# Placing the expert choices of layer 1's second sequence behind the multiplication of its cosines

## The chip, the core and the metric

The kernel runs on one core of one Trainium2 chip. The metric is the device time of that core in microseconds (us). All data are float32. The core has TensorE (PE in the profile, with PEld for its weight loads), VectorE (DVE), ScalarE (ACT), GpSimd (POOL) and SyncE (SP); each works through a stream of instructions in order, and waits at an instruction until the data and the buffers that it needs are there. SP issues loads and stores, POOL the gathers and scatters.

## The reference, cut to what matters

The input x is 4 sequences of 1024 tokens of width 256. Two layers follow one another, each of the same outer form:

```python
xn = layernorm(x)
s = attn(xn)                    # layer 0: a gated recurrence; layer 1: the attention below
x = x + s * silu(ffn(xn))
```

Layer 1's attention and its feed-forward part are

```python
proj = cos(theta) * cos(xn)                       # theta: one angle per column
attn = softmax(proj @ proj.T / 4)                 # per sequence
s = (attn @ proj) @ W_c.T + b_c

shared = (silu(xn @ sg.T) * (xn @ su.T)) @ sd.T   # 512 hidden columns
scores = sigmoid(xn @ router.T)                   # 16 experts in 4 groups
# two best groups by the sum of their two best scores, four best experts within
idx, w = topk(scores masked to those groups, 4);  w = w / sum(w)
routed = sum over the four: (w * silu(xn @ gate_e) * (xn @ up_e)) @ down_e   # 64 hidden columns
ffn = shared + routed
```

Layer 0's feed-forward part has 16 routed experts of 128 hidden columns, four per token, and no shared expert.

## The kernel before, in words

**Tiles.** A sequence is 8 tiles of 128 tokens, or two halves (q = 0, 1) of 512. Buffers come from pools of fixed size: "x" has 8 (gathered rows r, weighted sums y, layer 1's val, the dispatch's t_half), "t" has 1, "act" and "sg" 4, "o" 3; PSUM has four rings of two banks, "mm", "gu", "tp" and "acc". An instruction that takes a buffer waits for the last reader of what lay in it.

**Routed experts.** Tokens are scattered by POOL into rows sorted by expert (rows_in), the experts run over fixed blocks of these rows, and their results are gathered back. Layer 0's experts run over all sequences, in two groups of halves: (0,0), (0,1), (1,0) and (1,1), (2,0), (2,1), (3,0), (3,1), written (sequence, half). After them comes the combine (gated0, L773): per tile, a "piece": POOL gathers four rows per token (L730), DVE adds them weighted (one L795 of 0.25 to 0.35 us and three L797), and after four pieces ACT and DVE apply silu (L473, L474), DVE multiplies by the recurrence's output (L804) and adds to x (L806), and SP stores the half. So 12 pieces belong to the first group and 20 to the second.

**Layer 1 per sequence b.**
- route1(b) (L913), for each half that the combine has finished: layernorm statistics on DVE (L197, L198), the reciprocal root by Newton steps (L206 to L214), the scaling on ACT (L231), eight transposes on PE (L240), their copies into xnT (L242 on DVE, L244 on ACT), and a store of the normalized half to normed (SP). For b = 2 and 3 also a store of the transposed sequence to normedT. Then the router's products (L301), sigmoid (L317 on ACT), and about 40 small DVE instructions that choose the experts (L318 to L351, the choices), copies of the choices (em, L933) and of the normalized weights (L358 to L361, L934).
- places1(h) (L364 and what follows) for a pair of sequences: two PE products over the choices (L375, L377) and DVE instructions L381 to L448, which give each token its rows. There are two pairs, (0,1) and (2,3).
- dispatch1(h) (L943): POOL loads the normalized halves (L958), copies their places beside them (L959, L960) and scatters them (64 L587 for each pair).
- prep1(b) (L974): in four blocks of 512 columns, five DVE instructions each reduce the angles (L175 to L184, the cosine blocks); ACT takes the sine (L1002); DVE multiplies by cos(theta) (L1005, twice), which makes projT; PE multiplies by W_c into val (L1013, 16 products in PSUM "gu"), which ACT copies out (L1020). For b below 2 it uses the transposed tile that route1 left in `turned[b]`; for b = 2 and 3 it waits until route1(b) is emitted (`routed_done`) and loads normedT.
- attend(b) (L1025): scores L1066 in "mm", transposes L1074 where a block mirrors one already taken, ACT exponentials (L1078, L1082), products with val (L1098 in "acc"), then eviction of each half (sv, L1123 on DVE and a copy on ACT) and scaling (L1040, L1041, L1045).
- share(b) (L1134): products g in "mm" and u in "gu" (L1145), ACT and DVE (L473, L474, L1155), down products (L1161), eviction and store.
- experts1: the routed experts over both pairs, evictions L690, results stored by POOL (L1212); after them the rest of the layer.

**Order.** All these are generators. The main line (L1396 on) emits attend(0), share(0), attend(1), share(1), attend(2), share(2), then the routed experts. `run` (L892) advances a modelled clock after each of their steps, and lets the generators beside it (`Beside`, L872) emit what is due by then; a `yield` gives the modelled time until the next step (PIECE is 1, SETTLED 3). `combined` goes through the combine, `preparing` through prep1(b+1) beside attend(b) and share(b), and is finished before attend(b+1). `routing` goes in one line through route1(0), route1(1), places1(0), route1(2), route1(3), places1(1), dispatch1(0), dispatch1(1). Tile's scheduler fixes from this, before the run, the order of each engine's stream and the buffers.

The profile's line numbers are those of this kernel:

Of the kernel before, what the change touches and what calls it, by code (L numbers as in the profile page):

```python
# [52 lines left out]
PIECE = 1.0  # L53
# [10 lines left out]
def two_layer_kernel(  # L64
# [28 lines left out]
    def bank(tag, bufs):  # L93
        tag = side[0] if tag == "side" else tag
        return psum.tile([P, 512], F32, tag=tag, name=tag, bufs=bufs)


    def block(dram, b, q):


        if len(dram.shape) == 4:
            return dram[b, q].rearrange("p (c d) -> p c d", c=NS)
        return dram[b].rearrange("(c p) d -> p c d", p=P)[:, q * NS : (q + 1) * NS, :]
# [143 lines left out]
    def transposed_tile():  # L247
        return work.tile([P, KC, S], F32, tag="xnT", name="xnT", bufs=3)
# [28 lines left out]
    def two_of_four(v, tag):  # L277

        m = v.shape[1] // 4
        tt = nc.vector.tensor_tensor  # L280
        pair = v.rearrange("p (n two) -> p n two", two=2)
        hi = small.tile([P, 2 * m], F32, tag=f"hi{tag}", name=f"hi{tag}", bufs=1)
        lo = small.tile([P, 2 * m], F32, tag=f"lo{tag}", name=f"lo{tag}", bufs=1)
        tt(hi, pair[:, :, 0], pair[:, :, 1], ALU.max)
        tt(lo, pair[:, :, 0], pair[:, :, 1], ALU.min)
        hi2 = hi.rearrange("p (n two) -> p n two", two=2)
        lo2 = lo.rearrange("p (n two) -> p n two", two=2)
        first = small.tile([P, m], F32, tag=f"first{tag}", name=f"first{tag}", bufs=1)
        second = small.tile([P, m], F32, tag=f"second{tag}", name=f"second{tag}", bufs=1)
        rest = small.tile([P, m], F32, tag=f"rest{tag}", name=f"rest{tag}", bufs=1)  # L290
        tt(first, hi2[:, :, 0], hi2[:, :, 1], ALU.max)
        tt(second, hi2[:, :, 0], hi2[:, :, 1], ALU.min)
        tt(rest, lo2[:, :, 0], lo2[:, :, 1], ALU.max)
        tt(second, second, rest, ALU.max)
        return first, second

    def logits(lg, at, xnT, rw, tiles=range(NT)):

        for at, c in zip(range(at, 512, E), tiles):
            for kc in range(KC):  # L300
                nc.tensor.matmul(  # L301
                    lg[:, at : at + E],
                    lhsT=xnT[:, kc, c * P : (c + 1) * P],
                    rhs=rw[:, kc, :],
                    start=(kc == 0),
                    stop=(kc == KC - 1),
                )
        spent(len(tiles) * 0.44)

    def route(lg, nt, rb, masked_low):  # L310


        shape = [P, nt, E]
        flat = "p t e -> p (t e)"
        sc = small.tile(shape, F32, tag="sc", name="sc", bufs=1)

        nc.scalar.activation(sc.rearrange(flat), lg[:, 0 : nt * E], AF.Tanh, scale=0.5)  # L317
        nc.vector.tensor_scalar(sc, sc, 0.5, 0.5, ALU.mult, ALU.add)  # L318
        sb = small.tile(shape, F32, tag="sb", name="sb", bufs=1)
        nc.vector.tensor_tensor(sb, sc, rb.unsqueeze(1).to_broadcast(shape), ALU.add)  # L320
        yield PIECE
        first, second = two_of_four(sb.rearrange(flat), "e")
        yield PIECE
        gs = small.tile([P, nt, G], F32, tag="gs", name="gs", bufs=1)
        gflat = "p t g -> p (t g)"
        nc.vector.tensor_tensor(gs.rearrange(gflat), first, second, ALU.add)
        _, least = two_of_four(gs.rearrange(gflat), "g")
        yield PIECE
        gm = yield from chosen(gs, least.unsqueeze(2), 2, G)
        yield PIECE  # L330

        yield PIECE
        four = [P, nt, G, E // G]
        grouped = "p t (g k) -> p t g k"
        nc.vector.tensor_tensor(
            sb.rearrange(grouped, g=G), sb.rearrange(grouped, g=G), gm.unsqueeze(3).to_broadcast(four), ALU.mult
        )
        if masked_low:
            pen = small.tile([P, nt, G], F32, tag="pen", name="pen", bufs=1)
            nc.vector.tensor_scalar(pen, gm, BIG, -BIG, ALU.mult, ALU.add)  # L340
            nc.vector.tensor_tensor(
                sb.rearrange(grouped, g=G), sb.rearrange(grouped, g=G), pen.unsqueeze(3).to_broadcast(four), ALU.add
            )
        yield PIECE
        top = small.tile([P, nt, 8], F32, tag="top", name="top", bufs=1)
        for c in range(nt):
            nc.vector.max(top[:, c, :], sb[:, c, :])
        yield PIECE
        em = yield from chosen(sb, top[:, :, 3:4], 4, E)
        yield PIECE  # L350
        nc.vector.tensor_tensor(sc, sc, em, ALU.mult)  # L351
        return em, sc
# [220 lines left out]
    def spent(us):  # L573

        clock[0] += us
# [332 lines left out]
    em1 = small.tile([P, B * NT, E], F32, tag="em1", name="em1", bufs=1)  # L908
    comb1 = small.tile([P, B * NT, E], F32, tag="comb1", name="comb1", bufs=1)

    x1_halves = {b: [] for b in range(B)}

    def route1(b, tag):  # L913

        xnT = transposed_tile()
        for q in range(NQ):
            while len(x1_halves[b]) <= q:
                yield PIECE
            src, dst = x1_halves[b][q]
            part = [(xnT, q, src, dst)]  # L920
            scales = yield from norm_scales(part)
            yield from norm_applied(part, scales, tag)
            nc.sync.dma_start(out=block(normed, b, q), in_=dst)
        if b >= 2:
            nc.sync.dma_start(out=normedT[b], in_=xnT.rearrange("p k s -> p (k s)"))
        lg = bank(tag, 2)
        logits(lg, 0, xnT, r1w_sb)
        yield SETTLED
        if b < 2:
            turned[b] = xnT  # L930
        em, comb = yield from route(lg, NT, r1b_sb, True)
        ts = slice(b * NT, (b + 1) * NT)
        nc.vector.tensor_copy(em1[:, ts, :], em)  # L933
        nc.vector.tensor_copy(comb1[:, ts, :], normalized(comb))  # L934
# [39 lines left out]
    def prep1(b, tag):  # L974

        if b < 2:
            while b not in turned:
                yield PIECE
            xnT = turned[b]
        else:  # L980
            while b not in routed_done:
                yield PIECE
            xnT = transposed_tile()
            nc.sync.dma_start(out=xnT.rearrange("p k s -> p (k s)"), in_=normedT[b])
            there = clock[0] + LANDING
            while clock[0] < there:
                yield PIECE
        if b == 1:

            projT = [work.tile([P, QUAD, D + INFO], F32, tag="q", name="projT", bufs=QB) for _ in range(KC)]  # L990
            projT = [t.rearrange("p i d -> p (i d)")[:, 0:S] for t in projT]
        else:
            projT = work.tile([P, KC, S], F32, tag="big_a", name="projT", bufs=1)
            projT = [projT[:, kc, :] for kc in range(KC)]
        for kc in range(KC):
            for cols in (slice(0, TB), slice(TB, S)):
                k = work.tile([P, TB], F32, tag="t", name="k", bufs=1)
                for _ in cos_reduced(projT[kc][:, cols], xnT[:, kc, cols], k, TWO_PI_NORMED):
                    pass
                yield 2 * PIECE  # L1000
        for kc in range(KC):
            nc.scalar.activation(projT[kc], projT[kc], AF.Sin, bias=half_pi, scale=-1.0)  # L1002
        yield PIECE
        for kc in range(KC):
            nc.vector.tensor_scalar(projT[kc], projT[kc], cth[:, kc : kc + 1], None, ALU.mult)  # L1005
        yield 3 * SETTLED

        val = [xpool.tile([P, NS, D + INFO], F32, tag="x", name="val", bufs=XB)[:, :, 0:D] for _ in range(NQ)]
        for c in range(0, NT, 2):
            ps = bank(tag, 2)  # L1010
            for i in range(2):
                for kc in range(KC):
                    nc.tensor.matmul(  # L1013
                        ps[:, i * D : (i + 1) * D],
                        lhsT=projT[kc][:, (c + i) * P : (c + i + 1) * P],
                        rhs=wc_sb[:, kc, :],
                        start=(kc == 0),
                        stop=(kc == KC - 1),
                    )
            nc.scalar.copy(val[c // NS][:, c % NS : c % NS + 2, :], ps.rearrange("p (c d) -> p c d", d=D))  # L1020
            spent(1.7)
            yield PIECE
        ready[b] = xnT, projT, val
# [454 lines left out]
```

## Time and profile before

| | us |
|---|---|
| median of 9 runs | 1130.91 |
| lowest, highest | 1127.82, 1137.66 |
| profiled execution | 1132.52 |
| its span | 1130.8 |
| PE busy in it | 1028.2 |
| DVE busy | 650.2 |
| POOL busy | 568.0 |
| ACT busy | 463.9 |

The mean clock granted to TensorE in the profiled execution was 0.957 of full speed. The times of the trace count from the start of its span. In it, the choices of the second sequence stand around 514 to 541 on DVE, the multiplication L1005 of its cosines at 553.31, the first pair's places until 561; attend(2) starts at 702.72 on PE, and the routed experts of layer 1 at 790.2. POOL scatters layer 1's tokens from 628.69, and stores the first result (L1212) at 800.69.

A row of a timeline has start, length, engine, line, operation, output <- inputs, shapes and count, and, where the engine was idle before it, how long and what released it. Instructions of DVE overlap by some 0.1 us, so the distance of two starts is often a little less than the length that is shown. A product of float32 matrices is two MATMUL records; a product with 512 columns takes 0.86 us and one with 256 columns 0.43 us where PE is at full clock.

### The profile page before, as it was taken

To read this page: it belongs to the slowest core of one execution; us is meant where nothing else is said; L and a number is where in the kernel's file an instruction comes from. 1 tells how busy PE (TensorE), PEld (TensorE's weight loads), DVE (VectorE), ACT (ScalarE), POOL (GpSimd) and SP (SyncE) were. 2 spreads that over 40 slices of the span, in tenths; PEclk is the share of its full clock that TensorE was granted. 3 is DMA by queue.
4 is the path that set the end of the run, shared out by engine and by line. 5 is a ranking of instruction groups with operands and counts; after the bars stand their busy time and mean duration, and the time that the engine had idled before them with its cause. 6 is when DMAs were issued, how large, how long until landed. Compare 5 with 4: busy or idle time off the path is not lost.

```text
span 1130.8 us, 16114 instructions
## 1 busy us (share of the span) xinstructions
PE 1028.2 (91%) x4928; PEld 765.7 (68%) x4928; DVE 650.2 (57%) x1928; ACT 463.9 (41%) x1028; POOL 568.0 (50%) x589
## 2 busy tenths in 40 slices
PE   5679699999898899978599999999899999999997
PEld 4255368888677688665367765776677777776675
DVE  4867953333787733158876883034723437776666
ACT  3354364444455444321332611221745555553132
POOL 1277577721770000477253677777656666765000
PEclk9868799999999999989798989999999999999999
DMA  8997679999998587987246543564556579994871
GB/s 339 401 408 260 210 204 317 335 262 276 286 344 250 159 202 185 347 256 178 76 143 208 194 165 141 199 215 143 170 171 189 184 232 358 346 314 145 274 241 38
DMA packets 118994, 264.81 MB, mean 234 GB/s; under 512 B 14208, under 2 KB 71680, under 8 KB 117632
## 3 DMA queue, kind: packets, MB, share of 16 engines
q1 hardware_dynamic: 78256, 138.79, 39.3%
q0 software_dynamic: 27264, 75.86, 20.1%
q10 hardware_dynamic: 13392, 49.14, 12.5%
q8 instruction: 43, 0.70, 0.3%
q14 instruction: 39, 0.32, 0.1%
HBM read 119.34 MB, written 144.39 MB: 233 GB/s over the span
## 4 chain that ended last, share of the span: by engine, by line
PE 67%; DVE 19%; DMA 6%; issue 3%; POOL 2%; ACT 2%; DVEq 0%; POOLq 0%; ACTq 0%
PE gu L647 15%; PE acc L672 11%; PE acc L1098 7%; PE tp L635 6%; PE gu L1145 4%; PE mm L1066 4%; DMA r<-rows_out,row 4%; PE acc L1161 3%; PE mm L1145 3%; PE tp L664 3%; PE gu L1013 2%; DVE x_half L1250 2%; PE acc L301 2%; POOL r L730 2%; PE mm L519 1%
## 5 line engine op out<-in xcount | busy, mean ns | idle before, releaser
L730 POOL DMA_INDIRECT r<-rows_out,row x128 | 133.4, 1042 | 236.8 <-issue 154.9
L647 PE MATMUL gu<-w_sb,xT 128*128 x1280 | 239.6, 330 | 1.8 <-ACT xT L639 0.9
L647 PEld LDWEIGHTS gu<-w_sb,xT 128*128 128x128 f32 x1280 | 195.0, 193 | 16.6 <-issue 2.8
L1212 POOL DMA_INDIRECT results<-o,dest x160 | 159.5, 997 | 82.3 <-issue 28.5
L672 PE MATMUL acc<-w_sb,hT 128*128 (+1 forms) x640 | 180.2, 397 | 4.0 <-ACT hT L666 4.0
L587 POOL DMA_INDIRECT rows_in<-x_half,row x128 | 136.6, 1067 | 92.7 <-DVE stats L197 44.9
L474 DVE SCALAR_TENSOR_TENSOR h<-sg,gu 128x256 f32<-128x256 f32 (+1 forms) x160 | 56.0, 351 | 161.1 <-ACT sg L473 160.2
L587 POOL DMA_INDIRECT rows_in<-t_half,row x128 | 125.8, 983 | 40.6 <-issue 38.6
L672 PEld LDWEIGHTS acc<-w_sb,hT 128*128 128x128 f32 (+1 forms) x640 | 107.4, 189 | 32.0 <-issue 15.9
L1098 PE MATMUL acc<-val,es 128*128 128x256 f32 x512 | 125.9, 388 | 0.8 <-ACT es L1078 0.8
L639 ACT COPY xT<-tp 128x512 f32<-128x512 f32 x160 | 93.6, 586 | 74.7 <-PE tp L635 72.4
L1098 PEld LDWEIGHTS acc<-val,es 128*128 128x128 f32 x512 | 95.9, 195 | 23.8 <-issue 10.1
L635 PE MATMUL tp<-ident,xs 128*128 128x128 f32 x640 | 101.0, 281 | 0.0
L473 ACT ACTIVATE sg<-gu 128x256 f32<-128x256 f32 (+1 forms) x160 | 52.9, 331 | 115.0 <-PE gu L647 108.8
L635 PEld LDWEIGHTS tp<-ident,xs 128*128 128x128 f32 x640 | 74.4, 142 | 32.5 <-issue 18.5
L690 DVE COPY o<-acc 128x512 f32<-128x512 f32 x80 | 55.0, 688 | 63.2 <-PE acc L672 62.5
L664 PE MATMUL tp<-ident,h 128*128 128x128 f32 (+1 forms) x320 | 62.4, 277 | 9.2 <-DVE h L658 6.9
L1066 PE MATMUL mm<-projT 128*128 128x512 f32 (+3 forms) x192 | 70.6, 491 | 0.0
L666 ACT COPY hT<-tp 128x256 f32<-128x256 f32 (+1 forms) x160 | 58.5, 366 | 25.3 <-PE tp L664 23.7
L1145 PE MATMUL gu<-xnT,w_sb 128*128 128x512 f32 x128 | 61.9, 606 | 5.6 <-ACT val L1020 4.3
L1145 PE MATMUL mm<-xnT,w_sb 128*128 128x512 f32 x128 | 61.0, 601 | 1.0 <-DVE act L474 1.0
L1161 PE MATMUL acc<-w_sb,act 128*128 128x256 f32 x256 | 60.0, 381 | 0.7 <-DVE act L1155 0.7
(225 smaller groups left out, 1442.8 us busy)
## 6 DMA issues: line engine op xcount, KB each, us to landing
rows_in<-zeros SPq DMA_DIRECT2D x20, 1044.0 KB, 14.1
xs<-rows_in SPq DMA_DIRECT2D x40, 512.0 KB, 7.2
rows_out<-o ACTq DMA_DIRECT2D x40, 512.0 KB, 7.0
xs<-rows_in ACTq DMA_DIRECT2D x37, 522.0 KB, 4.7
r<-results SPq DMA_DIRECT2D x32, 512.0 KB, 6.7
rows_in<-zeros SPq DMA_DIRECT2D x1, 12288.0 KB
rows_in<-zeros SPq DMA_DIRECT2D x1, 8192.0 KB, 24.1
w_sb<-in_w_dram SPq DMA_DIRECT2D x4, 1536.0 KB, 16.2
```

What stands on the lines that cost most here:

```text
L587: nc.gpsimd.indirect_dma_start(out=view, out_offset=bass.IndirectOffsetOnAxis(ap=row[:, c0 + s, k : k + 1], axis=0), in_=tokens[:, s, :], ...
L635: nc.tensor.transpose(tp[:, at : at + P], xs[:, j % per * 2 + i, kc * P : (kc + 1) * P], ident)
L639: nc.scalar.copy(xT.rearrange("p i k t -> p (i k t)"), tp)
L647: nc.tensor.matmul(ps[:, i * 2 * hid : (i + 1) * 2 * hid], lhsT=xT[:, i, kc, :], rhs=w_sb[:, bass.ds(off + kc * 2 * hid, 2 * hid)], start= ...
L664: nc.tensor.transpose(tp[0:hid, i * P : (i + 1) * P], h[:, i, :], ident)
L672: nc.tensor.matmul(ps[:, i * D : (i + 1) * D], lhsT=hT[0:hid, i * P : (i + 1) * P], rhs=w_sb[0:hid, bass.ds(expert(2 * j + i) + 4 * hid, D ...
L730: nc.gpsimd.indirect_dma_start(out=r[:, k, :], out_offset=None, in_=rows_out[g], in_offset=bass.IndirectOffsetOnAxis(ap=row[:, c, k : k + ...
L1066: nc.tensor.matmul(ps[:, at:TB], lhsT=projT[kc][:, t * P : (t + 1) * P], rhs=projT[kc][:, q * TB + at : (q + 1) * TB], start=(kc == 0), st ...
L1098: nc.tensor.matmul(av[s // 2][:, (s % 2) * D : (s % 2 + 1) * D], lhsT=es[:, s * P : (s + 1) * P], rhs=val[t // NS][:, t % NS, :], start=(t ...
L1145: nc.tensor.matmul(ps, lhsT=w[:, kc, j * P : (j + 1) * P], rhs=xr[:, kc, :], start=(kc == 0), stop=(kc == KC - 1),)
L1161: nc.tensor.matmul(ys[s // 2][:, (s % 2) * D : (s % 2 + 1) * D], lhsT=h[:, s * P : (s + 1) * P], rhs=ds1_sb[:, j, :], start=(j == 0 and s ...
L1212: nc.gpsimd.indirect_dma_start(out=views[g - G1][QUAD * q + i], out_offset=bass.IndirectOffsetOnAxis(ap=dest[:, i : i + 1], axis=0), in_=o ...
```

## The change

A set of sequences is kept whose cosines have been multiplied. route1 for the second sequence (b = 1) now stops, after its router's products, until prep1(1) has emitted its multiplication; prep1 enters b in the set there. While it stops, it yields PIECE each time it is asked. No instruction is added or removed.

```diff
+    cosines = set()
     x1_halves = {b: [] for b in range(B)}
...
         yield SETTLED
         if b < 2:
             turned[b] = xnT
+
+        while b == 1 and b not in cosines:
+            yield PIECE
         em, comb = yield from route(lg, NT, r1b_sb, True)
...
         for kc in range(KC):
             nc.vector.tensor_scalar(projT[kc], projT[kc], cth[:, kc : kc + 1], None, ALU.mult)
+        cosines.add(b)
         yield 3 * SETTLED
```

Since `routing` is one line of generators, what follows route1(1) in it also follows the multiplication: the first pair's places, route1(2) and route1(3), the second pair's places, and the dispatch; and prep1(2), which waits for route1(2). The combine is a generator of its own and does not wait. The changed kernel's line numbers are larger by 1 from L911, by 4 from L932 and by 5 from L1006; the text gives those of before.

## Prediction

> **What bounds the kernel now.** I read first the page's busy shares and the 40 slices (28.3 us each), then the table of windows over the stretch in which layer 1's second sequence is prepared, then the timelines of PE and DVE there, and last the order in which both programs' instructions stand on each engine, which the scheduler fixes before the run.
>
> ```profile
> PE 1028.2 (91%) x4928; PEld 765.7 (68%) x4928; DVE 650.2 (57%) x1928; ACT 463.9 (41%) x1028; POOL 568.0 (50%) x589
> PE   5679699999898899978599999999899999999997
> ```
> ```profile
> 520.00:540.00 20.00, 13.78 (x44) 8.62 (x43) 20.00 (x71) 2.42 (x4) 15.55 (x15) 0.87 0.48 141
> 540.00:560.00 20.00, 12.33 (x30) 7.10 (x29) 19.49 (x68) 7.18 (x8) 5.29 (x6) 0.79 0.30 93
> ...
> 702.70:751.50 48.80, 48.80 (x211) 36.58 (x210) 3.72 (x10) 12.89 (x46) 36.54 (x47) 1.00 0.56 190
> 751.50:790.20 38.70, 38.70 (x123) 23.14 (x122) 16.70 (x31) 7.15 (x12) 29.54 (x31) 1.00 0.56 188
> ```
>
> PE bounds the whole (91%). In the second fence the columns after window and length are busy PE, PEld, DVE, ACT and POOL, then PE clock, DMA share and GB/s. From 520 to 560 DVE is the full engine (20.00 and 19.49 of 20) and PE idles 6.2 and 7.7 us. From 702.70 to 790.20, which are the third sequence's attention and shared expert, PE is full and DVE nearly idle. So DVE's order decides around 520 to 560, and PE wherever DVE has kept ahead.
>
> ```profile
> 538.16 1.22 PE L375 MATMUL tp<-em,before__110 128*128 128x256 f32 x2 [6.22 <-DVE em L933]
> 554.11 6.00 PE L1013 MATMUL gu<-wc_sb,projT 128*128 128x256 f32 x16 [6.68 <-DVE projT L1005]
> 566.11 3.40 PE L1145 MATMUL gu<-xnT,w_sb 128*128 128x512 f32 x4 [4.29 <-ACT val L1020]
> 570.21 3.62 PE L1013 MATMUL gu<-wc_sb,projT 128*128 128x256 f32 x16
> ```
>
> These are the stalls that the change touches: 6.22 us for the choices (em), 6.68 us for the multiplied cosines, 4.29 us for val's copies.
>
> **The change, part by part.** Nothing is added or removed; only places in the streams and buffers move. Second sequence's choices (L318 to L934) and the first group's places (L375 to L448) are emitted behind the multiplication L1005. In the generator chain `routing` stand behind them, and so move too, the layernorm and transposes of sequences 2 and 3, their stores to normed and normedT on SP, and the third sequence's preparation, which waits for them. The dispatch on POOL keeps its place there but waits for their data.
>
> *1. The head, a gain.* After the eviction at 514.30 DVE now has ahead of L1005: four cosine blocks of 0.33+0.33+3x0.60 = 2.46 us (starts in the timeline), 0.66 of it in idle time: 9.2; four L1045 at 0.40: 1.6; three combine pieces of 0.25+3x0.40: 4.35; four products of the shared expert at 0.60: 2.4; a combine's end (2x0.60+2x1.15): 3.5; the choices' first eight instructions: 0.8. Sum 22, so L1005 ends at 537.7, where before it ended at 554.6: 17 earlier. PE then does 8 val products (6.00, row 554.11), a u-product 1.7 and, held to 548.3 by a product queued behind the choices on DVE, the down product; then g, places, 8 val, g, u, g, u (0.86+1.0+3.45+0.86+3x1.72 = 11.3) to 559.6, and three downs and two g-u pairs (1.73+3.44+1.73+3.44+3.45 = 13.8). The first share ends at S = 573.4. Before, it ended at 592.4 with 5.5 of attention inside: 586.9. **Gain 13.5.**
>
> The Trainium skill, "TensorE: Matmul & The Clock Gate", Part 1, says that PE runs at half clock after an idle window of about 3.4 us, and warms after as much work. The rows agree in kind: 6.00 us after 6.68 of idleness, 3.62 for the same products warm. By the rule a restart costs about 1.7 us, by the rows 2.4; the sum goes by the rows.
>
> *2. What stands behind the wait, a loss.* In the changed DVE stream the eviction L1123 of the second attention's first half stands ahead of combine pieces 13 to 20, most of the places, and the layernorm of sequence 2. Before, they stood ahead of it and ran at 555 to 620. Such an eviction holds all:
>
> ```profile
> 477.74 0.69 DVE L1123 COPY sv<-acc 128x512 f32<-128x512 f32 x1 [18.18 <-PE acc L1098]
> 478.35 0.35 DVE L795 TENSOR_SCALAR y<-r,wk 128x256 f32<-128x256 f32 x1
> ```
>
> DVE waited 18.18 us, and the ready piece (L795) ran only after it. The attention alone takes PE 46.2 (702.72 to 751.5, less 2.6 of pulled-in share), its first eviction 25 after its start (729.43-702.72-1.7). So DVE is held to S+25. Piece 13 moreover writes a buffer of the x pool that held val, which PE reads last at S+36 (741.34-702.72-2.6).
>
> The same page, "Architectural detail", calls DVE's queue a strict FIFO of depth 8. This speaks against the change, and the two rows agree with the order (not with the depth, which no run here shows): by it everything behind the eviction waits as summed here; with free order the loss would be near nothing.
>
> *3. The chain that follows.* From S+36, link by link, each worked from rows of before:
> - pieces 13 to 17 (1.45 each), the rest of the places (L414 to L448, 552.23 to 561.2 without L1005) and the first layernorm statistics: 14.3, S+50.4; second eviction, rden, L1045 and Newton steps (0.2 each): 5.6, S+56;
> - third sequence's first half: ACT, transposes, copy 3.5 (616.58 to 620.15): S+59.5; second half's statistics, Newton and two L474: 5.5, S+65; silu end, transposes, copy: 6.7, S+71.7;
> - its logits and sigmoid 3.7 (row 508.54 and the idle row below): S+75.5; its choices with a piece or two between 13.0, where before they took 601.98 to 616.25 = 14.3: S+88.5.
>
> ```profile
> 601.98 0.23 DVE L318 TENSOR_SCALAR sc<-sc 128x128 f32<-128x128 f32 x1 [5.90 <-ACT sc L317]
> ...
> 616.25 0.23 DVE L934 COPY comb<-sc 128x128 f32<-128x128 f32 x1
> ```
>
> These choices end at 573.4+88.5 = 662 instead of 616: 46 late. Behind them, in series on DVE:
> - Newton 2.6, pieces and end of the fourth sequence's halves 4.0, statistics and Newton 4.5: S+99.6; two cosine blocks of 3.0 (640.62 to 643.61): S+105.6; copy, logits 4.6 and two more blocks 5.3: S+115.5; sin and the multiplication 3.7: S+119.2; choices to em 4.0 (656.61 to 660.6): S+123.2; places' products: S+125.
>
> PE meets this in the second share. Its stream there is: five g-products, L240 x16, L301, L240 x16, L301, val of the third sequence and the places, and only then the first u-product, since u takes its PSUM banks from the same two of "gu" as val. PE's work from S to the share's end is 46.2 + 38.7 + transposes, logits, val and places 18 = 103 us; it cannot run through, since everything behind L240 waits for the chain. After the places (8.9, 664.58 to 674.39) the first product is multiplied at S+134; left are 32 products at 0.43 and 16 at 0.86 (27.6) and 0.7: the share ends at S+162.5 = **735.9, before 702.7: 33.2 later**. From S to there it takes 162.5, before 702.7-586.9 = 115.8: 46.7 more, less the gain of 13.5.
>
> *4. What comes after.* Attention and share of sequence 2 take 87.5 with PE full and shift whole; the routed experts begin at 823 instead of 790.2. POOL's scatters (628.69 to 800.69 with pieces between) begin at about S+77 = 650 and end at 822; the first result is stored, and so POOL needed, some 10 after the experts begin, 834. They are hidden by the same delay. If the experts began earlier, they would not be (rival 3). Stores to normed on SP and loads of xs shift with them.
>
> **Sum.** The profiled execution took 1132.52, its span 1130.8, 1.7 more around it. 1130.8+33.2 = 1164.0; with 1.7, 1165.7. The profiled run lies 1.6 above the median 1130.91, so on the median's scale 1164.1: **1164**.
>
> **Unknown costs, from both sides.** The buffer wait of piece 13 does not show in before: at least 0 (covered by the eviction, chain 5 earlier by way of idle links), at most the 11 from S+25 to S+36; I take 11, since the same read of val is in the streams. Cold val products: 3.62 to 6.00, I take 6.00. S: 570 to 578, as DVE and PE alternate. DVE links: 4 less if they interleave as at 606 to 616. Low: 33.2-2.6-5-4-3 = 18.6, 1149. High: S +4.6, a clock of 0.8 over the share's remaining 28 (+5) and gathers landing late (+3, the row 492.56 waited 3.19): 46, 1177.
>
> **Rivals.**
> - *R1, faster.* The early multiplication keeps its 13.5 because the chain fits beside PE's 103 us. For it: DVE is busy only 9.66 of 20 in 680 to 700 and has room. Against: the eviction's place and the 28 instructions of L240 and L301 ahead of the u-products. It decides if the first multiplication after the u-products comes by S+88 (115.8-28.3) instead of S+134. Then 1130.9-13.5 = 1117. Chance 0.07.
> - *R2, same.* The stall only eats the gain: that multiplication comes at S+101 (88+13.5), 1131. Nothing in particular speaks for it. Chance 0.05.
> - *R3, POOL bounds instead.* The chain on DVE is shorter than summed, PE reaches the experts near 777, but scatters started 20 late end at 822. The three o buffers hold three pairs of 6.0 ((1033.1-797.4)/39, rows of L690), the first out 7.2 after the start, so PE is blocked from 777+7+18 = 802 and waits, with a result's store and landing, some 25: net +12, 1143. For it: POOL runs without a gap from 628.69 to 800.69 in before. Chance 0.14.
> - *R4, worse.* PE's waiting holds attention's own inputs too, or the order costs more in the experts: above 1178, about 1185. Chance 0.06.
> - *That the change does not do what it says* is excluded: the streams have L1005 ahead of the choices' rest.
>
> **How the numbers follow.** Forecast 1149 to 1178: 0.68; R3 0.14, R1 0.07, R2 0.05, R4 0.06. The range reaches from R3 to the forecast's upper end, 1143 to 1178, 0.82. A measurement of this kernel can tell about 0.3%, 3.4 us. Faster 0.07 (R1), same 0.05 (R2), slower 0.88.
>
> **What would show it.** In the profile after: L1005 of this sequence at about 536 and no 6.68 idle before its val products at the old place (step 1); a L1123 row on DVE with over 10 us idle, pieces after it, at about 598 (step 2); third sequence's choices near 650 to 662 (step 3); PE idle some 40 us or more between 620 and 720, before L240, L301, L1013 and L1145 (step 3); the experts' start near 823 with POOL's scatters ended before (step 4). Wrong would be the forecast if PE shows 9s through that stretch, or if most of the idle time stands before L635 or L672 on results that POOL has not moved.

## The result, and the profile after

The changed kernel takes 1167.82 us (median of 10 runs, 1162.62 to 1173.15), the kernel before 1130.36 (median of 31 runs). The ratio is 1.0325, with a 95% interval from 1.0305 to 1.0344: slower by 34 to 39 us, 37.5 in medians. The forecast was 1164, the range 1143 to 1178. Ratios here and below are of fast runs alone, those not more than 1.5% above the fastest of their kernel, while medians are of all runs, so the two can differ.

The profiled execution took 1171.58, its span 1169.9. The layer before the change already ran 4.0 us later in it: the first products with the shared expert's weights start at 461.20, and at 457.16 in the profile of before. The two programs have the same instructions up to there, so these 4 us are taken off where single steps are compared; the profiled run lies 3.8 above its median. That they belong to this one execution and not to the change is seen in e7 and e11 below, which also put work behind the cosines: the same products start at 457.08 and 457.32 there.

From the page, after: PE's share, and its 40 slices of 29.2 us.

```profile
PE 1036.7 (89%) x4928; PEld 772.9 (66%) x4928; DVE 650.9 (56%) x1928; ACT 462.0 (39%) x1026; POOL 565.0 (48%) x589
...
PE   5579699999799899987998349999999999999997
```

PE does the same work as before (1036.7 and 1028.2 us), but there is a hole of three slices, 8 3 4, at 614 to 702 us. The windows of the same profile show what is on both sides of it (columns as in the prediction):

```profile
520.00:540.00 20.00, 13.36 (x39) 6.95 (x37) 19.89 (x46) 6.17 (x10) 14.57 (x13) 0.90 0.51 143
540.00:560.00 20.00, 18.30 (x63) 13.53 (x64) 16.03 (x60) 5.59 (x8) 10.69 (x12) 0.84 0.47 150
560.00:580.00 20.00, 20.00 (x65) 11.87 (x64) 13.18 (x36) 5.12 (x10) 1.39 (x2) 1.00 0.23 80
580.00:600.00 20.00, 20.00 (x82) 14.45 (x81) 0.00 (x0) 5.12 (x20) 0.00 (x0) 1.00 0.04 17
...
660.00:680.00 20.00, 2.54 (x10) 1.46 (x10) 18.79 (x80) 4.32 (x9) 15.43 (x16) 0.50 0.68 235
680.00:700.00 20.00, 10.59 (x44) 9.24 (x43) 16.09 (x53) 5.50 (x8) 15.88 (x18) 0.50 0.57 198
```

The second half of that stretch before:

```profile
560.00:580.00 20.00, 15.71 (x55) 9.90 (x54) 11.76 (x36) 7.02 (x13) 4.54 (x4) 0.91 0.33 104
```

From 540 to 580 PE is busier than before (18.30 and 20.00 us of 20, against 12.33 and 15.71). From 580 to 600 DVE does nothing at all: 0.00 us, no instruction. From 660 to 700 it is the other way round: DVE is busy for 34.88 of 40 us, PE for 13.13, at a granted clock of 0.50. DVE's work was put off and then had to be done with PE waiting. PE's timeline in the hole, with what ended each wait:

```profile
541.56 6.01 PE L1018 MATMUL gu<-wc_sb,projT 128*128 128x256 f32 x16 [7.93 <-DVE projT L1009]
...
634.18 2.07 PE L1150 MATMUL mm<-xnT,w_sb 128*128 128x512 f32 x2 [5.77 <-DVE act L474]
...
671.60 2.17 PE L240 MATMUL tp<-ident,y 128*128 128x128 f32 x8 [17.27 <-ACT y L231]
679.63 2.17 PE L240 MATMUL tp<-ident,y 128*128 128x128 f32 x8 [5.86 <-ACT y L231]
682.47 7.01 PE L301 MATMUL tp<-r1w_sb,xnT 128*128 128x16 f32 x32 [0.68 <-ACT xnT L244]
698.22 4.63 PE L1018 MATMUL gu<-wc_sb,projT 128*128 128x256 f32 x10 [8.74 <-DVE projT L1009]
```

The first row is the gain: val of the second sequence starts at 541.56 instead of 554.11. The others are the loss: transposes and cosines of the third and fourth sequences, which PE has in its stream ahead of the second share's u-products. What holds DVE before them stands in its own timeline:

```profile
602.94 0.69 DVE L1128 COPY sv<-acc 128x512 f32<-128x512 f32 x1 [27.56 <-PE acc L1103]
610.45 0.17 DVE L1045 TENSOR_REDUCE rden<-den 128x4 f32<-128x16 f32 x1 [6.82 <-ACT es L1083]
...
614.85 0.62 DVE L795 TENSOR_SCALAR y<-r,wk 128x256 f32<-128x256 f32 x2 [2.31 <-PE acc L1103]
...
654.68 0.23 DVE L318 TENSOR_SCALAR sc<-sc 128x128 f32<-128x128 f32 x1 [4.00 <-ACT sc L317]
```

The second attention starts on PE at 577.94. For 27.56 us DVE waits at its eviction, then for the exponentials, and the first combine piece (L795) is at last released by PE L1103, a product with val: 36.9 us after the attention's start. The third sequence's choices (L318) start at 654.68, 76.7 after it. Before, they started at 601.98.

### The profile page after: what moved, and what is told of

It reads as the page before. It is cut to its first block, busy times and chain, and to the rows that moved or that the text cites. A ratio compares the mean times of both kernels' runs of the same rounds, so it can differ in the third digit from the quotient of the medians.

```text
span 1169.9 us, 16120 instructions
## 1 busy us (share of the span) xinstructions
PE 1036.7 (89%) x4928; PEld 772.9 (66%) x4928; DVE 650.9 (56%) x1928; ACT 462.0 (39%) x1026; POOL 565.0 (48%) x589
## 4 chain that ended last, share of the span: by engine, by line
PE 63%; DVE 19%; DMA 9%; issue 4%; POOL 3%; ACT 2%; DVEq 0%; ACTq 0%; POOLq 0%
PE gu L647 14%; PE acc L672 10%; PE acc L1103 6%; DMA r<-rows_out,row 6%; PE tp L635 5%; PE acc L1166 4%; PE gu L1150 4%; PE mm L1071 4%; PE mm L1150 4%; PE tp L664 3%; POOL r L730 2%; PE acc L301 2%; DMA rows_out<-o 1%; PE mm L519 1%; DVE stats L197 1%
## 5 line engine op out<-in xcount | busy, mean ns | idle before, releaser
L730 POOL DMA_INDIRECT r<-rows_out,row x128 | 130.2, 1017 | 275.7 <-issue 159.2
L1103 PE MATMUL acc<-val,es 128*128 128x256 f32 x512 | 124.4, 388 | 0.8 <-ACT es L1083 0.8
L1103 PEld LDWEIGHTS acc<-val,es 128*128 128x128 f32 x512 | 96.4, 194 | 24.4 <-issue 10.5
L1166 PEld LDWEIGHTS acc<-w_sb,act 128*128 128x128 f32 x256 | 48.6, 190 | 18.8 <-issue 9.3
```

Source lines behind the costliest of these rows:

```text
L730: nc.gpsimd.indirect_dma_start(out=r[:, k, :], out_offset=None, in_=rows_out[g], in_offset=bass.IndirectOffsetOnAxis(ap=row[:, c, k : k + ...
L1103: nc.tensor.matmul(av[s // 2][:, (s % 2) * D : (s % 2 + 1) * D], lhsT=es[:, s * P : (s + 1) * P], rhs=val[t // NS][:, t % NS, :], start=(t ...
L1166: nc.tensor.matmul(ys[s // 2][:, (s % 2) * D : (s % 2 + 1) * D], lhsT=h[:, s * P : (s + 1) * P], rhs=ds1_sb[:, j, :], start=(j == 0 and s ...
```

## The experiments

**Theory T.** The loss comes from a buffer. The earlier cosines let val of the second sequence be laid into the x pool before the combine's sum y of half (3,0). In the changed program the first half of val gets the very buffer that y of that half takes next; in the program before they lie in different ones (read from the two built programs, not from a trace). So piece 13 can't be written until the second attention has read val, and the theory has it that the scheduler for this reason puts pieces 13 to 20 and what follows them on DVE behind the attention's evictions. PE then waits in the second share, since its u-products stand behind val of the third sequence.

**Rivals.** F: DVE is held by the eviction as such. C: the late choices of the second sequence cost. W: the wait as such costs, since it holds everything behind it in the line of generators. P: POOL's late scatters cost.

The chips that the runs fell on were not alike. Beside e7, e11 and e12 the kernel before took 1127.8, 1126.7 and 1127.8 us, as in the first runs. Beside e1 to e6 and e8 to e10 it took 1444 to 1460 (of what that was, see the last section). Ratios are to the kernel before on the same chip; times of the two kinds are not compared with each other. e1 to e4 ran on one of these chips, e5 and e8 to e10 on a second, e6 on a third.

**e1, e5, e8, e11: val of the second sequence apart.**

```diff
-        val = [xpool.tile(... tag="x", name="val", bufs=XB)[:, :, 0:D] for _ in range(NQ)]
+        if b == 1:
+            both = work.tile([P, NT, D], F32, tag="big_a", name="val", bufs=1)
+            val = [both[:, q * NS : (q + 1) * NS, :] for q in range(NQ)]
+        else:
+            val = [xpool.tile(... tag="x", name="val", bufs=XB)[:, :, 0:D] for _ in range(NQ)]
```

> The changed kernel with one more edit: the second sequence's val lies in the buffer big_a, which is free between the first sequence's attention and the third's cosines, and no longer takes two of the x pool's eight. The wait for the cosines stays. Theory T (the buffer): the loss comes from the first buffer of val, which the combine takes next for the sum of half (3,0); so pieces 13 to 20, and all of the layernorm and choices that follow them, stand behind the second attention. Without that, pieces 13 to 20 and the third sequence's choices run beside the attention (choices started by some 30 us after the attention's start instead of 77), the gain at the head stays, and the loss goes: 1110 to 1132, likeliest 1118, with POOL's scatters then ending last. Rival W (the wait itself): what costs is that choices, places and the two later sequences stand behind the multiplication in the line of generators; they still do, so 1150 to 1168.

> The kernel of e1 once more, since in e1's runs every kernel, the one before too, took some 1440 to 1470 us, and what they wait for there is not what the first runs show. Numbers for a chip on which the kernel before takes about 1131. Theory T (val's place in the x pool pushes pieces 13 to 20 behind the second attention): the loss goes and the head's gain stays, 1110 to 1132, likeliest 1118; the third sequence's choices start on DVE within 30 us of the second attention's start, where the changed kernel took 77. Rival W (the wait itself, that holds choices, places and two sequences behind the multiplication): 1150 to 1168, and those choices start 60 us or more after it.

> The kernel of e1 and e5 under the first conditions again (beside e7 the kernel before took 1127.8). Theory T: loss gone, head's gain kept: 1110 to 1132, likeliest 1118, the third sequence's choices within 30 us of the second attention's start. Rival W (the wait itself): 1150 to 1168.

> The kernel of e1, e5 and e8, for a chip on which the kernel before takes about 1128, as beside e7. Theory T: 1110 to 1132, likeliest 1118, choices of the third sequence within 30 us of the second attention's start. Rival W (the wait itself): 1150 to 1168. On a chip where the kernel before takes 1440 or more, both as in e8: a ratio to before of 1.00, against 1.012 of the changed kernel in e6.

| run | median, us | before, same chip | quotient of the medians | ratio (95%) |
|---|---|---|---|---|
| e1 | 1452.5 | 1443.9 | 1.0060 | 0.9985 (0.9933 to 1.0036) |
| e5 | 1454.3 | 1445.9 | 1.0058 | 1.0014 (0.9970 to 1.0058) |
| e8 | 1455.2 | 1450.4 | 1.0033 | 1.0040 (1.0006 to 1.0075) |
| e11 | 1130.0 | 1126.7 | 1.0029 | 1.0029 (1.0007 to 1.0050) |

In e11 the loss of 37 us is gone but for 3, with the wait still in place. W falls. DVE's rows in e11, a piece of half (3,0), the end of that half (L804), the third sequence's choices, and the second attention's first eviction (L1132 there), which now comes last:

```profile
583.21 0.34 DVE L795 TENSOR_SCALAR y<-r,wk 128x256 f32<-128x256 f32 x1
...
596.05 1.22 DVE L804 SCALAR_TENSOR_TENSOR y<-y,g_half 128x1024 f32<-128x1024 f32 x1
...
604.65 0.23 DVE L318 TENSOR_SCALAR sc<-sc 128x128 f32<-128x128 f32 x1 [3.94 <-ACT sc L317]
...
610.83 0.68 DVE L1132 COPY sv<-acc 128x512 f32<-128x512 f32 x1
```

The second attention starts at 576.30 there, so the third sequence's choices come 28.3 us after it, against 76.7 in the changed kernel. But the likeliest time that theory T gave, 1118, was not reached. The second attention starts 10.6 earlier than the 586.9 worked out for before, and the third at 703.97, 1.3 later than before: what was won was lost between the two. PE's timeline in e11 has the place:

```profile
642.94 3.70 PE L1154 MATMUL mm<-xnT,w_sb 128*128 128x512 f32 x8 [1.27 <-DVE act L474]
...
653.42 2.42 PE L1154 MATMUL mm<-xnT,w_sb 128*128 128x512 f32 x4 [3.27 <-DVE act L474]
657.56 6.59 PE L1022 MATMUL gu<-wc_sb,projT 128*128 128x256 f32 x20 [1.73 <-DVE projT L1009]
...
674.62 3.15 PE L1170 MATMUL acc<-w_sb,act 128*128 128x256 f32 x8 [3.59 <-DVE act L1164]
```

In the whole stretch from 576.3 to 704.0 PE is busy for 113.3 of 127.7 us, so it idles 14.4 us, 9.9 of it from 640 on, in the second share, where val of the third sequence (L1022, at 657.56) stands ahead of the u-products. The edit may bring part of this itself: by the program the third sequence's cosines also lie in big_a, and must wait until val has been read there. How much that costs was not measured on this kind of chip.

**e4, e10: the same place for val, in the kernel before (control).**

> The kernel before with the same place for val as in e1 (big_a). Theory T: there, pieces 13 to 20 did not stand behind val, so the place gains nothing; the third sequence's cosines must now wait for the end of the second attention, which they began before: 1130 to 1139. If this were much faster than before, the buffer would be a gain of its own and e1 would not tell of the change.

> The kernel of e4 under the first conditions: the kernel before with val in big_a, as a control for e8. Theory T: no gain, 1126 to 1139, since there the place of val held no piece. If it were faster by 8 or more, e8 would not tell of the change.

1471.2 against 1443.9 (ratio 1.0190, 1.0128 to 1.0252) and 1476.3 against 1450.4 (1.0182, 1.0127 to 1.0237). The place gains nothing by itself; on those chips it costs 26 to 27 us, where at most 9 were expected. Why it costs so much there was not looked into, and on a chip of the first kind it was not tried.

**e3: the eviction taken off DVE.**

```diff
-                if s == 0:
+                if s == 0 and (b, q) != (1, 0):
                     nc.vector.tensor_copy(to, av[s // 2])
```

> The changed kernel with the eviction of the second attention's first half moved whole from DVE to ACT. Theory T: piece 13 waits for val's buffer (36.9 us after the attention's start) whatever stands before it, so nothing is won: 1164 to 1172. Rival F (DVE held by the eviction that stands ahead, to 25 us after the attention's start): what stands behind starts up to 12 us earlier: 1152 to 1160.

1466.6 against 1443.9, ratio 1.0177 (1.0114 to 1.0239). The numbers of the expectation don't hold on this chip; the trace answers. DVE in e3:

```profile
770.88 0.17 DVE L1045 TENSOR_REDUCE rden<-den 128x4 f32<-128x16 f32 x1 [35.08 <-ACT es L1083]
...
775.27 0.62 DVE L795 TENSOR_SCALAR y<-r,wk 128x256 f32<-128x256 f32 x2 [2.31 <-PE acc L1103]
```

The eviction is gone from DVE, and the piece starts as late: at 775.27, 36.9 us after the attention's start at 738.37, released by PE's product with val as before. F falls: the eviction is not what holds the pieces. Another instruction of the same attention (L1045, which waits for the exponentials) still stands ahead of them, so e3 alone doesn't say why the stream has this order; e11 does, where val's place is the one edit and the pieces of half (3,0) stand ahead of the eviction.

**e7: the choices early, the rest behind the cosines.**

```diff
-        while b == 1 and b not in cosines:
-            yield PIECE
         em, comb = yield from route(lg, NT, r1b_sb, True)
...
     def places1(h):
+        while h == 0 and 1 not in cosines:
+            yield PIECE
```

> The choices of the second sequence go back to their old place, ahead of the multiplication; only what follows them in the line of generators (the first pair's places and the two later sequences) still waits for the cosines. The cosines come early enough that val is still laid where the sum of half (3,0) goes next. Theory T (val's place holds piece 13 and all behind it): the first piece after the second attention's first eviction is again released by PE's product with val, some 37 us after that attention's start, and the time stays 15 to 40 above the kernel before on the same chip. Rival C (the late choices are what costs): the time goes back to that of the kernel before, within 8.

1163.5 against 1127.8, ratio 1.0310 (1.0289 to 1.0330). The choices of the second sequence are back at 512 to 539 on DVE, and nearly the whole loss stays (35.7 us in medians, of 37.5). C falls. The piece is held by the same product:

```profile
512.65 0.23 DVE L318 TENSOR_SCALAR sc<-sc 128x128 f32<-128x128 f32 x1 [3.21 <-ACT sc L317]
...
539.35 0.21 DVE L935 COPY em<-gt 128x128 f32<-128x128 f32 x1
...
601.89 0.69 DVE L1128 COPY sv<-acc 128x512 f32<-128x512 f32 x1 [25.85 <-PE acc L1103]
...
613.79 0.62 DVE L795 TENSOR_SCALAR y<-r,wk 128x256 f32<-128x256 f32 x2 [2.30 <-PE acc L1103]
```

**e2, e9: the third sequence's val in another PSUM ring.**

```diff
-        preparing = Beside(prep1(b + 1, "gu")) if b < 2 else Beside(loads1())
+        preparing = Beside(prep1(b + 1, ("gu", "tp")[b])) if b < 2 else Beside(loads1())
```

> The changed kernel with the third sequence's val products in the PSUM ring tp instead of gu, so that the second share's u-products no longer stand behind them. Theory T: DVE's chain stays as late as in the changed kernel, but PE does the second share meanwhile; the third attention starts some 30 us earlier. POOL's scatters still end near 831, and the experts, who reach them near 798, wait for a store: 1138 to 1155, likeliest 1149. Rival P (POOL's late scatters alone are the loss): 1165 to 1170, since they start no earlier. If PE's order were the whole loss and POOL nothing: 1134 to 1138.

> The kernel of e2 under the first conditions. Theory T: pieces stay held (the choices of the third sequence again some 77 us after the second attention's start), but PE does the second share's u-products meanwhile: 1138 to 1155, likeliest 1149, the experts waiting for a store. Rival P (POOL's late scatters alone are the loss): 1162 to 1170.

1449.8 against 1443.9 (0.9970, 0.9915 to 1.0026; quotient of the medians 1.0041) and 1453.6 against 1450.4 (0.9956, 0.9904 to 1.0008; medians 1.0022). In e2's trace the pieces are held as in the changed kernel:

```profile
778.61 0.62 DVE L795 TENSOR_SCALAR y<-r,wk 128x256 f32<-128x256 f32 x2 [2.31 <-PE acc L1103]
...
820.88 0.23 DVE L318 TENSOR_SCALAR sc<-sc 128x128 f32<-128x128 f32 x1 [4.13 <-ACT sc L317]
```

The choices of the third sequence come 81 us after the second attention's start at 739.8, and yet most of the loss is gone: on the same chip e3, which mended nothing, took 1466.6. So the order on PE looks like the second half of the mechanism: DVE's lateness costs where the u-products stand behind it. POOL's scatters begin no earlier by this edit (825.3 to 1021 us in e2, 820.8 to 1001 in e3), which speaks against P. This edit alone was not run on a chip of the first kind, so what it is worth there, and whether the experts then wait for a store, was not seen; e12 below has it together with the other edit.

**e6: the changed kernel on such a chip.**

> The changed kernel itself, unedited, to have it beside the kernel before on the same chip and under the same conditions as the other runs here. If the kernel before takes about 1131 again, both theories expect 1163 to 1173. If it takes some 1440, as beside e1 to e5, theory T (val's place holds pieces 13 to 20 until the second attention has read val) and rival W both expect it slower than before, by 15 to 40; the trace must then show the first L795 after the second attention's eviction released by PE L1103.

1478.7 against 1460.4, ratio 1.0120 (1.0075 to 1.0166). This, and e3's 1.0177, are the numbers that e1, e5, e8 (0.9985 to 1.0040) and e2, e9 (0.9970, 0.9956) are to be held against. By the medians it is 1.0125 and 1.0157 against 1.0033 to 1.0060 and 1.0041, 1.0022: each edit gives back some 0.7 to 2% there, though e6 was on another chip than they. The mechanism is in the trace as in the first profile: attention from 740.7, piece released by PE L1103 at 777.6 (36.9), choices at 818.1 (77.4).

**e12: both edits.**

> Both edits together on the changed kernel: val of the second sequence in big_a, so that no piece is held, and the third sequence's val products in the ring tp, so that the second share's u-products need not wait for them. Theory T with the reading of e11 (there the early start of the second attention, 576 against 587, was lost again because PE idled 14 us in the second share, where u stands behind the third sequence's late val): with u free, PE runs through from the second attention, about 105 to 110 us to the third, which then starts at 681 to 687 instead of 703; POOL's scatters end near 783 as in e11 and hold nothing. On a chip where the kernel before takes about 1128: 1105 to 1118, ratio 0.98 to 0.99. Rival S (the head start is lost in any case to DVE and to the scatters): 1125 to 1132, ratio 1.00. Where the kernel before takes 1440 or more: ratio below those of e8 and e9 for theory T, between them for rival S.

1110.6 against 1127.8, ratio 0.9863 (0.9822 to 0.9904): some 15 us (11 to 20) faster than the kernel before, with the change's wait in place. Choices of the third sequence, PE's slices, and the stretch from the second attention (571.8) to the third (683.5):

```profile
600.17 0.23 DVE L318 TENSOR_SCALAR sc<-sc 128x128 f32<-128x128 f32 x1 [3.92 <-ACT sc L317]
```
```profile
PE   5669699999899799989899999999899999999997
```
```profile
571.80:683.50 111.70, 108.28 (x465) 76.50 (x465) 89.74 (x331) 42.68 (x94) 67.44 (x75) 1.00 0.51 178
```

PE is busy for 108.28 of 111.70 us; the stretch took 127.7 in e11 and 115.8 before. The third attention starts at 683.5 instead of 702.7, of which 2.9 are an early run (the first products with the shared expert's weights start at 454.31, not 457.16). S falls: the head start is not lost to DVE or to the scatters. The ring alone was not tried in the kernel before. By an estimate from the rows it had at most 1.8+5.7 = 7.5 us to win in this stretch there: PE idles for 1.8 of 115.8 us, and its 114.0 us of work at a granted clock of 0.94 are 5.7 more than the 108.3 of e12 at 1.00. So by this estimate at least half of the 15 comes from the early start of the second attention.

## Why the prediction was right

The time lay 3.8 us above the forecast (1167.82 and 1164), on the side forecast. Point by point (S is the start of the second attention, 577.94 in the profile after):

- **The head (step 1).** L1005 was expected to end at 537.7; it ended at 542.2, of which 4.0 is the late run: 538.2. The second attention was expected at 573.4; it came at 577.94, without the 4.0 at 573.9. The gain of 13.5 was 13.0.
- **The wait (step 2).** Eviction at S+25: S+25.0. Piece 13 at S+36: S+36.9. The 11 us between them, taken between bounds of 0 and 11, were there in full; DVE first waited for the exponentials, then for val.
- **The chain (step 3).** Places' end S+50.4: S+50.0. The third sequence's first shift S+56: S+56.1. Its choices from S+75.5 to S+88.5: S+76.7 to S+89.3. Em of the fourth S+123.2: S+124.5. First multiplication by u on DVE S+134: S+135.4. Third attention S+162.5: S+163.7 (741.66). Not one link is off by more than 1.4 us.
- **After it (step 4).** 87.5 us to the experts: 829.15-741.66 = 87.5. The scatters began at 659.9 and ended at 832.5 (655.9 and 828.5 without the 4.0), not 650 and 822, and hid all the same: the first result was stored at 837.4, released by DVE and not by the scatters:

```profile
831.52 0.96 POOL L587 DMA_INDIRECT rows_in<-t_half,row  x1 [0.31 <-issue]
837.36 0.95 POOL L1217 DMA_INDIRECT results<-o,dest  x1 [4.88 <-DVE h L474]
```

- **Sum.** 33.2 expected; 829.15-790.21 = 38.9 at the experts' start, 34.9 without the 4.0. In medians it is 37.5, 4 above the forecast. The late start belongs to one execution and can't explain a difference of medians, and the profiled run of before lies 2.2 above its own median too; where the 4 lie is not settled by one trace of each.

Some figures of the working don't come out of their rows. The colder val products cost 6.00-3.62 = 2.4, not 2.6, in the lower bound; a clock of 0.8 over 28 us costs 7, not 5, in the upper one, which so comes to 1179 and not 1177 or 1178; and DVE was not nearly idle through the third share (16.70 of 38.70 us). None of these enters the forecast.

What the prediction weighed less well is which of the two things in step 2 is the cause. It put the eviction's place in the stream first and took the buffer for an addition of 11 us. e3 and e11 show that the buffer is the cause and the eviction's place its consequence: without the eviction the piece comes as late (36.9), and with val elsewhere the pieces go ahead of it. For the sum it made no difference, since the order of the stream was read as it stood.

R1's 13.5 of gain was real; its condition, DVE's chain beside PE's work, was missed by the buffer and by PE's order, and e12, where both are mended, gets 1111. R3 (POOL bounds) was not met, and in e12 the scatters end at 777 and the experts begin at 771.0, with PE busy for 25.15 of the 26 us from 764 to 790.

The clock: in the hole PE was granted 0.50 (windows 660 to 700), where it was busy for 13.13 of 40 us, and 1.00 from 560 to 600, where it was busy throughout. 32 records of L301 took 7.01 us in the hole; the 32 of the second sequence took 3.72 in the profile of before (at 508.54). The Trainium skill, "TensorE: Matmul & The Clock Gate", Part 1, says that "the default state is throttled, and activity releases the throttle"; the rows agree. From the second attention to the third PE was busy for 121.1 us at a mean granted clock of 0.81, and before for 114.0 at 0.94, with 465 records in both.

## What to carry to other kernels

When work is moved earlier, look at what buffers it takes earlier: a pool that several loops share hands its next buffer to whoever comes first, and one long-lived tile can so hold a loop that has nothing to do with the change. In the streams this looks like a badly placed instruction (here an eviction ahead of the pieces), and moving that instruction mended nothing here; the release of the first instruction behind it names the buffer's last reader. A gain at one place is kept only if nothing behind it on the full engine waits for the engine that fell behind: here the u-products stood behind val of the next sequence because both took their banks from one PSUM ring, and another ring, with val's place mended, brought 1130.0 down to 1110.6.

## What the runs showed of the hardware that was not expected

The same kernel, before, took 1130 us in the first runs, 1127 to 1128 beside e7, e11 and e12 on two chips, and 1444 to 1460 on three others. In the traces from these three, stretches of some 30 us recur in which PE, DVE and ACT do next to nothing while POOL goes on issuing. The same 29.4 us in the changed kernel, in the first profile and then in e6:

```profile
87.60:117.00 29.40, 26.73 (x80) 13.82 (x79) 22.91 (x72) 15.21 (x25) 23.61 (x20) 0.88 0.65 242
```
```profile
87.60:117.00 29.40, 0.00 (x0) 0.00 (x0) 0.00 (x0) 0.00 (x0) 19.09 (x20) 0.50 0.65 237
```

PE had 80 records there in the one and none in the other, POOL 20 and 20, and the DMA engines moved 242 and 237 GB/s. The trace puts such waits down to "another core or an unknown queue" (15 to 20% of the chain in the nine traces from those chips; the five others don't have it). What it is was not tried and stays open. What a change is worth is not the same on them: the ratio of the changed kernel was 1.0325 on the first kind of chip and 1.0120 in e6.
